# A gated retention layer with a ternary feed-forward on one core: Down's weights scaled by GpSimd alone and stored in more steps, another pace for one group's attention, and retention's norms in two lots

## The chip, the core and the metric

The kernel runs on one core of a Trainium2 chip. A core has five engines that run side by side and wait for one another only where data or buffers ask for it: TensorE (PE in the profile; PEld is its loading of weights), VectorE (DVE), ScalarE (ACT), GpSimd (POOL) and SyncE (SP), which issues most of the DMA transfers. Each engine works through its own instructions in a fixed order; an instruction that has to wait holds up all that stand behind it on that engine.

The metric is the time of one execution in microseconds on the device. Before the change it is 2254.69 us, the median of 3 runs (2254.12 to 2256.78).

## The reference

64 sequences of 128 tokens with 512 features pass through one layer. `k` and `v` of the attention are both the context `ctx`.

```python
def xattn(x, k, v, Wh, wg_w, wo_w, gn_gamma, gn_beta):      # 4 heads of 128
    Q, K, V = xh @ Wh, kh @ Wh, vh @ Wh                     # per head
    scores = einsum('bshe,bthe->bhst', Q, K) / sqrt(hd)
    masked = scores * Dn                                    # fixed decay masks
    A = maximum(abs(masked.sum(axis=0)), 1.0)               # summed over all 64 sequences
    O = einsum('hst,bthe->bshe', A, V).reshape(b, s, dim)
    Y = (O - mu) / sqrt(var + GN_EPS) * gn_gamma + gn_beta  # norm over the 512 features
    W = relu(x @ wg_w)
    return W * Y @ wo_w

def ffn(x, gate_w, up_w, down_w, gate_s, up_s, down_s):     # 512 -> 1408 -> 512
    g = (x @ gate_w.T) * gate_s
    u = (x @ up_w.T) * up_s
    return (silu(g) * u) @ down_w.T * down_s

x = x + tanh(g_xattn[0]) * xattn(layernorm(x), ctx, ctx, ...)
x = x + tanh(g_ffn[0]) * ffn(layernorm(x), ...)
```

The attention matrix `A` sums over all sequences before its absolute value is taken. So the scores of every sequence have to be there before any retention output can be made, and the kernel passes over the data twice.

## The kernel before

The 64 sequences are worked through in 16 groups of 4 (`NG`, `GB`), 512 tokens at a time. The large matrix products are done by a scheme in the manner of Strassen and Winograd: seven products of half-size blocks instead of eight, with sums and differences of the blocks formed beforehand (`combine_a` for weights, `combine_b` for tokens), and, for Down, sums of the weight tiles after a longer list (`W_SUMS`, `W_SUMS3`).

**Pass 1** (the loop over `g` that begins with `pending = None`) does for each group: `prepare` (the first layer norm; `bn` on VectorE, the power -1/2 on GpSimd in `inv_std`, then `xn`, a transpose on TensorE and a copy into `xnT`), `scores` for the group before, and `project` (the gate W) for the group before. Beside it runs `prepare_weights`, a generator that is asked once a group, from group 2 on (`next(weights, None)`), and that prepares the weights of pass 2 in nine parts: Wo (`load_wo`, `sum_wo`), five blocks of gate and up (`load_gu`, `sum_gu`; `NJ` is 5) and Down in three (`load_down`, `sum_down`). A part is loaded into one of two buffers (tag `raw`), summed on GpSimd, and stored to a scratch tensor in DRAM when the generator is asked the next time. In `sum_down`, L431 to L447, each of the 8 half tiles (6 in the third part) is first multiplied by Down's scale `ds`. Where `DOWN_SIGN` is positive, GpSimd does it (L436); where it is negative, VectorE does it with a factor of -1 (L438). GpSimd's 18 (or 12) sums follow; those beyond slot 15 go to the tile `more` (`dn_t` in the profile). The first two parts leave as two stores each (L481: `raw`, 2 MB, and `more`, 1.25 MB), the third as twenty stores of 128 KB (L487), with a pause after every seventh. What SP issues within one request stands behind the last load of `x` issued before (`tc.issue_after(last_load[0].ins)`); GpSimd's and VectorE's instructions are not bound in this way.

The tile `ds` shares its tag `wo`, with 3 buffers, with `gram`, `decay` and, in pass 2, with the loaded tiles `wo_w` (L727).

**Pass 2** runs, for each group, `ffn`, and beside it the attention of the next group (`attended`) and the retention of the group after that (`next_retention`, `retention`). `ffn` goes through a remainder block and then, for each of five blocks `j`, seven products in this order, with one `yield` after each: GS1 into `bank_f`; GA12 into `bank_a`, whose halves `hidden` (L879 on ScalarE, L880 on VectorE) turns into `h`; GS2 into `bank_c`; GA11 of the next block into `bank_a`; GS3, GS4 and GA22. After them come the 24 steps of Down (L1006). So `bank_a` is filled again two products after `hidden` began to read it.

`retention` makes four products (`po`, L652), copies them to `o`, normalises the four sequences (`bn` L251 and L252, `inv_std` L246 on VectorE and L247 on GpSimd, `normalised` L279, `square_transposed` L263), and sends the result through DRAM to turn it round (`moved`, L269 and L272). It then yields `WAIT` = 8 times, multiplies by gamma on ScalarE (L702), and multiplies W by it on GpSimd and VectorE (L711). `attended` makes seven products with Wo (L730), adds them to `x_t` (L741), and does the second layer norm in the same manner.

**The order of the work** has two sources. `interleave` mixes the generators: each has a number of steps, and the one whose next step is the smallest share of its number goes next. `ffn` has 50 (`FFN_STEPS`); the chain of attention and retention has `int(n_steps * 1.4)`. That is the order in which the program is written down. A planner then orders each engine's instructions by priority in that order, with durations of its own, so that an instruction can come earlier than it is written where its engine would otherwise be idle: the first load of Wo's weights, which belongs to pass 2, is issued at 243 us in the middle of pass 1.

In the first round of pass 2 (`g == 0`) the chain is longer: the rest of `retention` of group 1 (its four products are already done), `attended` of group 1, and `retention` of group 2.

Of the kernel before, what the change touches and what calls it, by code (L numbers as in the profile page):

```python
# [10 lines left out]
F32 = mybir.dt.float32  # L11
AF = mybir.ActivationFunctionType
ALU = mybir.AluOpType
# [22 lines left out]
DOWN_SIGN = (-1, -1, 1, 1, -1, 1, 1, 1)  # L36
# [84 lines left out]
def chain(*gens):  # L121
    for gen in gens:
        yield from gen
# [3 lines left out]
def flamingo_gated_layer(  # L127
# [21 lines left out]
    nc = tc.nc  # L149
    P = 128  # L150
    B, S, DIM = x.shape
# [8 lines left out]
    HN = DIM // 2  # L160
    KC = NC // 2
    NJ = NI // 2
# [179 lines left out]
    once = pass1.enter_context(tc.tile_pool(name="once", bufs=1))  # L342
# [39 lines left out]
    decay = att.tile([P, H, S], F32, tag="wo", name="decay", bufs=3)  # L382
    ds = att.tile([P, DIM], F32, tag="wo", name="ds", bufs=3)

    def constants():

        nc.sync.dma_start(out=ds, in_=down_s.partition_broadcast(P))
        nc.sync.dma_start(out=decay, in_=decayT)
        nc.sync.dma_start(out=gamma_sb, in_=gamma.rearrange("(c p) -> p c", p=P))
        nc.sync.dma_start(out=beta_sb, in_=beta.rearrange("(c p) -> p c", p=P))  # L390
        nc.sync.dma_start(out=gs_sb, in_=gate_s)
        nc.sync.dma_start(out=us_sb, in_=up_s)

        cols = slice(REST * P, INTER)
        for m, mat, k in ((GA11, gateT, 0), (GA12, gateT, 1), (7, upT, 0), (GA22, upT, 1)):
            nc.sync.dma_start(
                out=gu_rest[:, m],
                in_=mat[k * HN : (k + 1) * HN, cols].rearrange("(c p) i -> p c i", p=P),
            )
# [8 lines left out]
    def sum_wo(raw):  # L408

        nc.vector.tensor_scalar_mul(ds, ds, tanh_g[:, 1:2])  # L410
        nc.vector.tensor_scalar_mul(raw, raw, tanh_g[:, 0:1])
        t = once.tile([P, 4, KC, HN], F32, tag="sums", name="wo_t")
        b = (
            raw[:, 0:KC, 0:HN], raw[:, 0:KC, HN:DIM], raw[:, KC:NC, 0:HN], raw[:, KC:NC, HN:DIM],
        )
        combine_b(nc.gpsimd, [t[:, i] for i in range(4)], *b)
        return [
            (wo_scr[m], src)
            for m, src in zip(range(7), (b[0], b[2], b[3], t[:, 0], t[:, 1], t[:, 2], t[:, 3]))
        ]  # L420
# [10 lines left out]
    def sum_down(n, raw):  # L431

        for i in range(2 * len(DOWN_QUADS[n])):
            scale = ds[:, (i % 2) * HN : (i % 2 + 1) * HN]
            if DOWN_SIGN[i] > 0:
                nc.gpsimd.tensor_tensor(raw[:, i], raw[:, i], scale, ALU.mult)  # L436
            else:
                nc.vector.scalar_tensor_tensor(  # L438
                    raw[:, i], raw[:, i], -1.0, scale, ALU.mult, ALU.mult
                )  # L440
        more = once.tile([P, 10, HN], F32, tag="sums", name="dn_t")
        slots = [raw[:, i] for i in range(16)] + [more[:, i] for i in range(10)]
        sum_tiles(nc.gpsimd, slots, W_SUMS if n < 2 else W_SUMS3)
        if n == 2:
            rest_weights()
            return [(dn_scr[place, :, n], slots[i]) for i, place in W_PLACES3]
        return [  # L447
            (dn_scr[0:16, :, n].rearrange("m p e -> p m e"), raw),
            (dn_scr[16:26, :, n].rearrange("m p e -> p m e"), more),
        ]  # L450
# [20 lines left out]
    def prepare_weights():  # L471


        parts = [(load_wo, sum_wo)]
        parts += [(partial(load_gu, j), partial(sum_gu, j)) for j in range(NJ)]
        parts += [(partial(load_down, n), partial(sum_down, n)) for n in range(3)]
        raw, stores = parts[0][0](), []
        yield
        for n, (_, sums) in enumerate(parts):
            for dst, src in stores:  # L480
                nc.sync.dma_start(out=dst, in_=src)  # L481
            stores = sums(raw)
            if n + 1 < len(parts):
                raw = parts[n + 1][0]()
            yield
        for n, (dst, src) in enumerate(stores):
            nc.sync.dma_start(out=dst, in_=src)  # L487
            if n % 7 == 6:
                yield

    def rest_weights():
# [98 lines left out]
    pending = None  # L590
    weights = prepare_weights()
    for g in range(NG):
# [16 lines left out]
        steps = 3 if g == NG - 1 else 7  # L609
# [35 lines left out]
    def retention(g, v, ws):  # L645

        helper = nc.vector if g < 3 else nc.gpsimd

        o = att.tile([P, GB, H, P], F32, tag="yT", name="o")
        for h in range(H):  # L650
            po = ps_mm.tile([P, GB, P], F32, tag="mm", name="po")
            nc.tensor.matmul(  # L652
                po, lhsT=attn[:, h, :], rhs=v[:, h, :, :], start=True, stop=True
            )
            if h % 2:
                nc.vector.tensor_copy(o[:, :, h, :], po)
            else:
                nc.scalar.copy(o[:, :, h, :], po)
            yield
        if g:  # L660
            sq = att.tile([P, NQ, NC, GB, SQ], F32, tag="sq", name="sq")
        ons = []
        for j in range(GB):
            oj = o[:, j].rearrange("p h e -> p (h e)")
            mv = stat.tile([P, 2], F32, tag="mv", name="mv")
            bn(mv, oj)
            rs = stat.tile([P, 1], F32, tag="rs", name="rs")
            inv_std(rs, mv[:, 1:2], GN_EPS, 1)
            if g:
                square_transposed(sq, j, normalised(oj, mv[:, 0:1], rs))  # L670
            else:
                nc.vector.tensor_scalar(oj, oj, mv[:, 0:1], rs, ALU.subtract, ALU.mult)
                ons.append(oj)
        if g == 0:
            for q in range(2):
                tok = slice(q * HT, (q + 1) * HT)
                for d in range(2):
                    pt = ps_mm.tile([P, KC, HT], F32, tag="mm", name="pt")
                    for c in range(KC):
                        e = (d * KC + c) * P  # L680
                        for i in range(2):
                            nc.tensor.transpose(
                                pt[:, c, i * P : (i + 1) * P], ons[2 * q + i][:, e : e + P], ident
                            )
                    y = att.tile([P, KC, HT], F32, tag="xn", name="y", bufs=2)
                    for c in range(KC):
                        e = d * KC + c
                        nc.scalar.activation(
                            y[:, c, :], pt[:, c, :], AF.Identity,
                            scale=gamma_sb[:, e : e + 1], bias=beta_sb[:, e : e + 1],  # L690
                        )
                    (helper if d else nc.gpsimd).tensor_tensor(
                        ws[q][:, d], ws[q][:, d], y, ALU.mult
                    )
                    yield
            return
        yT = att.tile([P, NQ, NC, GB, SQ], F32, tag="yT", name="yT")
        moved(yT, sq, sq_scr[0][g % 2])
        for _ in range(WAIT):
            yield  # L700
        for e in range(NC):
            nc.scalar.activation(  # L702
                yT[:, :, e], yT[:, :, e], AF.Identity,
                scale=gamma_sb[:, e : e + 1], bias=beta_sb[:, e : e + 1],
            )
        yield
        for d in range(2):
            for q in range(2):
                for k in range(KC):
                    w = ws[q][:, d, k, :].rearrange("p (g i b) -> p i g b", i=NQ, b=SQ)  # L710
                    (helper if d else nc.gpsimd).tensor_tensor(  # L711
                        w, w, yT[:, :, d * KC + k, q * 2 : q * 2 + 2, :], ALU.mult
                    )
            yield
# [80 lines left out]
            moved(x1nT, sq, sq_scr[1][g % 2])  # L795

    WAIT = 8
    RET_STEPS = 4 + WAIT + 2
    ATT_STEPS = 8 + GB

    def new_x1nT():
# [256 lines left out]
    for g in range(NG - 1):  # L1058
        x_t = x_next.pop(0)
        x1nT = new_x1nT()  # L1060
        if g + 2 < NG:
            x_next.append(load_x(g + 2))
        steps = [attended(g + 1, x_t, ws, x1nT)] if g else [second]
        n_steps = ATT_STEPS + RET_STEPS
        if g == 0:
            steps.append(late_attended(1, x_t, x1nT))
            n_steps += RET_STEPS - 4
        if g + 2 < NG:
            steps.append(next_retention(g + 2))
        interleave(  # L1070
            (ffn(*pending), FFN_STEPS), (chain(*steps), int(n_steps * 1.4)),
        )
        with tc.issue_after(mid_down[0].ins):
            tokens = combine_tokens(nc.vector, x1nT)
        pending = (g + 1, x_t, x1nT, tokens)
# [59 lines left out]
```

## Time and profile before

| what | value |
|---|---|
| median of 3 runs | 2254.69 us (2254.12 to 2256.78) |
| the profiled execution's own time | 2253.64 us |
| its span, first to last instruction | 2251.8 us |
| busy: TensorE, VectorE, ScalarE, GpSimd | 2218.9, 1190.2, 603.3, 654.0 us |
| pass 1 up to the turn, 0 to 404 us: TensorE busy | 390.3 us |
| turn to pass 2, 404 to 440 us: TensorE busy | 32.7 of 36 us |
| a later group of pass 2, e.g. 624 to 738 us: TensorE busy | 113.3 of 114 us |
| GpSimd around the three parts of Down: 181 to 206, 206 to 230, 230 to 254 us | busy 20.7, 10.3, 18.0 us |

The profile is of one execution. A timeline row gives the start in us from the span's start, the duration in us, the engine, the line, the operation, the tile written and the tiles read, the shape, how many instructions are merged into the row (x8), and in brackets how long the engine was idle before it and what ended that. A row "A <- B: 9.6, 13, 0.9" among the waits says that A's engine was idle for B's sake for 9.6 us in total, 13 times, at most 0.9 us. In the chain of waits a row gives start, duration and what the last instruction was, at that time, waiting for. fp32 matmuls of 128x128 with 256 columns appear as two instructions each; within a row they start some 0.216 us apart, and a row of eight, one of the seven block products, is followed by the next 1.73 us after its start.

### The profile page before, as it was taken

To read this page: it belongs to the slowest core of one execution; us is meant where nothing else is said; L and a number is where in the kernel's file an instruction comes from. 1 tells how busy PE (TensorE), PEld (TensorE's weight loads), DVE (VectorE), ACT (ScalarE), POOL (GpSimd) and SP (SyncE) were. 2 spreads that over 40 slices of the span, in tenths; PEclk is the share of its full clock that TensorE was granted. 3 is DMA by queue.
4 is the path that set the end of the run, shared out by engine and by line. 5 is a ranking of instruction groups with operands and counts; after the bars stand their busy time and mean duration, and the time that the engine had idled before them with its cause. 6 is when DMAs were issued, how large, how long until landed. Compare 5 with 4: busy or idle time off the path is not lost.

```text
span 2251.8 us, 28752 instructions
## 1 busy us (share of the span) xinstructions
PE 2218.9 (99%) x10112; PEld 1889.7 (84%) x10112; DVE 1190.2 (53%) x2863; ACT 603.3 (27%) x1132; POOL 654.0 (29%) x1038
## 2 busy tenths in 40 slices
PE   8999999999999999999999999999999999999999
PEld 7878787778888888888888888888888888888888
DVE  6456543646454646464646464646464646454524
ACT  3444445322222222222222222222221212121221
POOL 4125300240323333333333333323232324141220
PEclk9999999999999999999999999999999999999999
DMA  9788855678777777777777777777777777766654
GB/s 300 263 279 308 287 190 176 253 240 260 255 269 240 265 249 256 258 248 266 247 267 236 257 247 266 239 262 243 268 237 269 236 272 233 280 205 243 223 184 145
DMA packets 216863, 558.46 MB, mean 248 GB/s; under 512 B 21264, under 2 KB 62992, under 8 KB 199952
## 3 DMA queue, kind: packets, MB, share of 16 engines
q1 hardware_dynamic: 211296, 539.58, 70.9%
q10 hardware_dynamic: 5424, 17.04, 2.0%
q8 instruction: 81, 1.33, 0.2%
q14 instruction: 62, 0.51, 0.1%
HBM read 454.31 MB, written 102.24 MB: 247 GB/s over the span
## 4 chain that ended last, share of the span: by engine, by line
PE 84%; DVE 6%; DMA 5%; POOL 3%; issue 1%; SPq 1%; ACT 0%; ACTq 0%; DVEq 0%; POOLq 0%
PE bank_c L287 18%; PE bank_a L287 12%; PE bank_c L1006 9%; PE bank_b L1006 6%; PE bank_f L287 6%; PE bank_b L287 6%; PE bank_f L1006 4%; PE bank_a L1006 4%; PE by L730 3%; PE sv L538 3%; PE bx L730 3%; PE bz L730 2%; PE po L652 2%; DMA gu_scr<-gu_raw 2%; DVE st L251 2%; PE bank_c L890 2%
## 5 line engine op out<-in xcount | busy, mean ns | idle before, releaser
L287 PE MATMUL bank_c<-tcomb,gu 128*128 128x256 f32 x1920 | 454.9, 380 | 0.7 <-DVE c L965 0.7
L287 PEld LDWEIGHTS bank_c<-tcomb,gu 128*128 128x128 f32 x1920 | 363.3, 190 | 59.3 <-issue 6.7
L335 POOL TENSOR_TENSOR h<-h 128x128 f32<-128x128 f32 x576 | 253.2, 470 | 398.5 <-DVE h L880 282.1
L287 PE MATMUL bank_a<-x1nT,gu 128*128 128x256 f32 x1280 | 305.5, 381 | 11.2 <-DVE h L880 9.6
L287 PEld LDWEIGHTS bank_a<-x1nT,gu 128*128 128x128 f32 x1280 | 241.8, 190 | 62.2 <-DVE h L880 14.8
L1006 PE MATMUL bank_c<-dn_w,h 128*128 128x256 f32 x896 | 211.7, 379 | 0.0
L1006 PEld LDWEIGHTS bank_c<-dn_w,h 128*128 128x128 f32 x896 | 170.2, 190 | 23.2
L879 ACT ACTIVATE sil<-c,gs_sb 128x256 f32<-128x256 f32 x176 | 89.3, 508 | 336.4 <-DVE c L965 171.7
L965 DVE TENSOR_TENSOR c<-bank_c,m 128x512 f32<-128x512 f32 x80 | 55.3, 691 | 219.5 <-PE bank_c L287 219.5
L247 POOL TENSOR_TENSOR rs<-ve,mhalf 128x1 f32<-128x1 f32 x128 | 73.4, 585 | 322.7 <-DVE ve L246 209.8
L711 POOL TENSOR_TENSOR w_t<-w_t,yT 128x256 f32<-128x256 f32 x112 | 91.6, 847 | 258.0 <-ACT yT L702 258.0
L741 POOL TENSOR_TENSOR x_t<-x_t,m 128x512 f32<-128x512 f32 x48 | 62.1, 1323 | 341.4 <-ACT m L751 341.4
L1006 PE MATMUL bank_b<-dn_w,h 128*128 128x256 f32 x640 | 156.4, 379 | 0.0
L335 DVE TENSOR_TENSOR h<-h 128x128 f32<-128x128 f32 x608 | 152.8, 312 | 4.3
L287 PE MATMUL bank_f<-tcomb,gu 128*128 128x256 f32 x640 | 151.2, 379 | 0.0
L287 PE MATMUL bank_b<-x1nT,gu 128*128 128x256 f32 x640 | 151.2, 379 | 0.0
L287 PEld LDWEIGHTS bank_b<-x1nT,gu 128*128 128x128 f32 x640 | 121.6, 190 | 22.1 <-issue 6.2
L287 PEld LDWEIGHTS bank_f<-tcomb,gu 128*128 128x128 f32 x640 | 121.6, 190 | 17.0 <-issue 0.5
L1006 PEld LDWEIGHTS bank_b<-dn_w,h 128*128 128x128 f32 x640 | 121.6, 190 | 16.5
L251 DVE BATCH_NORM_STATS2 st<-x_t 128x6 f32<-128x512 f32 x128 | 83.7, 682 | 79.3 <-DMA x_t<-in_x_dram 78.2
L538 PE MATMUL sv<-qw,c_t 128*128 128x256 f32 x512 | 122.0, 383 | 3.3 <-DVE xnT L513 3.3
L1026 DVE TENSOR_TENSOR x_t<-x_t,bank_c 128x256 f32<-128x256 f32 x192 | 77.8, 420 | 86.9 <-PE bank_c L1006 86.8
(150 smaller groups left out, 3260.8 us busy)
## 6 DMA issues: line engine op xcount, KB each, us to landing
dn_w<-dn_scr SPq DMA_DIRECT2D x320, 384.0 KB, 4.9
gu<-gu_scr SPq DMA_DIRECT2D x80, 1024.0 KB, 7.8
gu<-gu_scr SPq DMA_DIRECT2D x80, 768.0 KB, 5.9
x_t<-in_x_dram SPq DMA_DIRECT2D x62, 512.0 KB, 5.3
sq_scr<-sq SPq DMA_DIRECT2D x30, 1024.0 KB, 4.8
wo_w<-wo_scr SPq DMA_DIRECT2D x112, 256.0 KB, 3.6
dn_w<-dn_scr SPq DMA_DIRECT2D x96, 256.0 KB, 5.2
c_t<-in_ctxT_dram SPq DMA_DIRECT2D x64, 256.0 KB, 4.9
```

Source lines behind the costliest of these rows:

```text
L247: nc.gpsimd.tensor_tensor(dst, ve, mhalf[:, :n], ALU.pow)
L251: nc.vector.bn_stats(st, src)
L287: nc.tensor.matmul(out, lhsT=w[:, s, k, :], rhs=x_k, start=(start and s == 0 and k == 0), stop=(s == 1 and k == KC - 1), skip_group_check= ...
L335: engine.tensor_tensor(slots[to], slots[a], slots[b], ALU.add if sign == "+" else ALU.subtract)
L538: nc.tensor.matmul(sv[:, 0 : 2 + i : 1 + i, :], lhsT=c_t[j][:, h, :], rhs=qw[:, h, j : GB + 1 : GB - j, :], start=(i == 0), stop=(i == 1), ...
L711: (helper if d else nc.gpsimd).tensor_tensor(w, w, yT[:, :, d * KC + k, q * 2 : q * 2 + 2, :], ALU.mult)
L730: nc.tensor.matmul(bank[:, i * HN : (i + 1) * HN], lhsT=lhs[:, k, i * P : (i + 1) * P], rhs=w[:, k, :], start=(start and i == 0 and k == 0 ...
L741: engine.tensor_tensor(dst, dst, src.rearrange("p (b d) -> p b d", b=2), ALU.add)
L879: nc.scalar.activation(sil, gate, AF.Silu, scale=gs_sb[:, i : i + 1])
L965: nc.vector.tensor_add(c22, bank_c, m5)
L1006: last_down[0] = nc.tensor.matmul(places[acc], lhsT=hq[q][:, a, :], rhs=dn[n][:, q, :], start=start, stop=True, skip_group_check=True,)
L1026: add = nc.vector.tensor_tensor(dst, dst, places[acc], ALU.add if sign > 0 else ALU.subtract)
```

## The change

- In `sum_down` all half tiles are multiplied on GpSimd. A second tile, `minus_ds`, holds the negated scale; it is made once, in `sum_wo`, on VectorE. It lies in the pool `once` and not under the tag `wo`.
- In `prepare_weights` the two stores of Down's first part, and those of the second, are issued at two requests instead of one: the generator yields after the first of them. The twenty stores of the third part pause after every tenth instead of every seventh. The generator thereby has 14 steps instead of 13, for the 14 requests that pass 1 makes.
- In `retention`, for all groups but the first, a `yield` stands after the norms of the first two sequences, so that the four norms are written down in two lots with other work between them. `RET_STEPS` counts one more.
- The chain's number of steps in the first round of pass 2 is `int(37 * 1.05)` = 38 instead of `int(36 * 1.4)` = 50; in later rounds it is 37 instead of 36, by the additional step.

```diff
+    minus_ds = once.tile([P, DIM], F32, name="minus_ds")
...
     def sum_wo(raw):
 
         nc.vector.tensor_scalar_mul(ds, ds, tanh_g[:, 1:2])
+        nc.vector.tensor_scalar_mul(minus_ds, ds, -1.0)
...
     def sum_down(n, raw):
 
         for i in range(2 * len(DOWN_QUADS[n])):
-            scale = ds[:, (i % 2) * HN : (i % 2 + 1) * HN]
-            if DOWN_SIGN[i] > 0:
-                nc.gpsimd.tensor_tensor(raw[:, i], raw[:, i], scale, ALU.mult)
-            else:
-                nc.vector.scalar_tensor_tensor(
-                    raw[:, i], raw[:, i], -1.0, scale, ALU.mult, ALU.mult
-                )
+            scale = (ds if DOWN_SIGN[i] > 0 else minus_ds)[:, (i % 2) * HN : (i % 2 + 1) * HN]
+            nc.gpsimd.tensor_tensor(raw[:, i], raw[:, i], scale, ALU.mult)
...
         for n, (_, sums) in enumerate(parts):
-            for dst, src in stores:
+            for i, (dst, src) in enumerate(stores):
                 nc.sync.dma_start(out=dst, in_=src)
+                if n > NJ + 1 and i == 0:
+                    yield
             stores = sums(raw)
             if n + 1 < len(parts):
                 raw = parts[n + 1][0]()
             yield
         for n, (dst, src) in enumerate(stores):
             nc.sync.dma_start(out=dst, in_=src)
-            if n % 7 == 6:
+            if n % 10 == 9:
                 yield
...
             else:
                 nc.vector.tensor_scalar(oj, oj, mv[:, 0:1], rs, ALU.subtract, ALU.mult)
                 ons.append(oj)
+            if g and j == 1:
+                yield
         if g == 0:
...
     WAIT = 8
-    RET_STEPS = 4 + WAIT + 2
+    RET_STEPS = 5 + WAIT + 2
     ATT_STEPS = 8 + GB
...
         if g == 0:
             steps.append(late_attended(1, x_t, x1nT))
-            n_steps += RET_STEPS - 4
+            n_steps += RET_STEPS - 5
         if g + 2 < NG:
             steps.append(next_retention(g + 2))
         interleave(
-            (ffn(*pending), FFN_STEPS), (chain(*steps), int(n_steps * 1.4)),
+            (ffn(*pending), FFN_STEPS), (chain(*steps), int(n_steps * (1.4 if g else 1.05))),
         )
```

## The prediction

> **What bounds the kernel.** I read the page first (busy times), then TensorE's waits, then the timeline and the chain of waits around each of them, then SyncE's waits.
>
> ```profile
> PE 2218.9 (99%) x10112; PEld 1889.7 (84%) x10112; DVE 1190.2 (53%) x2863; ACT 603.3 (27%) x1132; POOL 654.0 (29%) x1038
> ```
>
> TensorE is the bound. No matmul is added or removed, so the change can only alter TensorE's idle time, some 33 us (2251.8 - 2218.9), and the half-speed matmuls that follow a long pause. TensorE's waits (who, for whom: us, times, longest):
>
> ```profile
> PE bank_a L287 <- DVE h L880: 9.6, 13, 0.9
> ...
> PE sv L538 <- DVE xnT L513: 3.3, 1, 3.3
> PE bx L730 <- POOL w_t L711: 2.5, 2, 1.5
> ```
>
> The other entries lie at the start, at the turn from pass 1 to pass 2, or are under 0.9 us. The three differ in kind.
>
> *The first comes once in each of 13 groups* (feed-forward of groups 1 to 13). Timeline of one:
>
> ```profile
> 734.12 1.30 DVE L263 STREAM_TRANSPOSE sq<-xn 128x512 f32<-128x512 f32 x2
> 734.68 1.89 PE L287 MATMUL bank_c<-tcomb,gu 128*128 128x256 f32 x8
> 734.95 0.47 ACT L879 ACTIVATE sil<-bank_a,gs_sb 128x256 f32<-128x256 f32 x1 [1.20 <-PE bank_a L287]
> ...
> 736.12 0.67 DVE L279 TENSOR_SCALAR xn<-o,mv,rs 128x512 f32<-128x512 f32 x1 [0.21 <-POOL rs L247]
> 736.77 0.47 DVE L880 SCALAR_TENSOR_TENSOR h<-bank_a,us_sb,sil 128x256 f32<-128x256 f32 x1
> 737.30 1.99 PE L287 MATMUL bank_a<-x1nT,gu 128*128 128x256 f32 x8 [0.72 <-DVE h L880]
> ...
> 738.47 0.67 DVE L279 TENSOR_SCALAR xn<-o,mv,rs 128x512 f32<-128x512 f32 x1 [0.61 <-POOL rs L247]
> ```
>
> A product takes 1.73 us from start to start (eight matmuls; neighbouring rows). `bank_a` could be refilled at 734.68 + 1.73 = 736.41, once VectorE's `h` has read it. `h` has its input at 735.42 (734.95 + 0.47) and takes 0.47, so starting by 735.9 costs nothing. It starts at 736.77, because the four norms of retention (L251 to L263) occupy VectorE from 728.98 to 739.9. TensorE loses 0.89 us, and 0.10 more in the product after the pause (1.83 to the next start): 0.99. In the first of the 13 groups the same rows give 1.21 (2.84 + 1.83 - 3.46). Together 12 x 0.99 + 1.21 = **13.1 us**.
>
> *The second comes once, in pass 1.* The chain of waits through it:
>
> ```profile
> 215.20 13.48 DMA dn_scr<-dn_raw
> ...
> 228.69 4.04 DMA dn_raw<-in_downT_dram
> ...
> 236.25 0.87 DVE dn_raw L438
> ...
> 245.34 6.01 DMA x_t<-in_x_dram
> ...
> 254.24 3.50 PE sv L538 x8
> ```
>
> Two stores of Down's first part leave together (2 MB and 1.25 MB). The load of the third part waits for their buffer, VectorE's negating multiply (L438) waits for the load, and all else of VectorE waits behind it. SyncE's waits show the next link:
>
> ```profile
> SPq L727 <- DVE dn_raw L438: 5.9, 1, 5.9
> SPq L727 <- POOL dn_raw L436: 5.8, 1, 5.8
> ```
>
> The first load of Wo's weights sits in SP's queue from 231.2 to 243.0, because its slot is that of `ds`, which the late multiplies still read; `x_t` and `c_t` queue behind it. TensorE loses 3.49 us before 254.24 (250.75 was possible), 1.61 because those eight matmuls run at half clock (3.34 to the next start instead of 1.73), and 0.77 and 0.61 at 235.36 and 241.58, where VectorE was late: **6.5 us**.
>
> *The third*, at 472 to 478, feed-forward of group 0: bx waits for gating on GpSimd behind eight sums, 1.20 + 1.63 us, 1.9 in slow matmuls after it; with 0.9 at 498, **5.6 us**.
>
> **The change, part by part.** *Scaling on GpSimd alone.* VectorE loses nine multiplies of 0.426 (median; 3.8 us) and their waits for loads (13.6 + 4.9 us in that line's waits). GpSimd gains 9 x 0.729 = 6.6 us (its like row; at the row's longest, 1.179, 10.6). One VectorE multiply for `minus_ds` (0.54, by the 128x512 row of L279) lies in the idle time before 60 us. The cover is GpSimd's idle time: 20.7 us busy of the 25 around Down's first part (181 to 206), under 6.1 in each of the groups before it. With three multiplies more that part needs about 23 of 24 us. What waits behind is `rstd` for the next group; at 200.91 it followed these sums and was first read at 209.3, so 2.2 us more are covered, and over 8 would show. I take 0; bounds: 0 to +2.
>
> [...]
>
> *Stores in more steps.* The generator is asked once a group, from group 2. Asked for the 9th time (group 10) it now issues only the 2 MB store; the 1.25 MB store and the third part's load come in group 11, the second part's stores in 12 and 13, and the twenty small ones as ten and ten in groups 14 and 15 (before: 7, 7, 6 in 12 to 14). Each batch stands in SP's queue behind that group's last `x_t` load, and all 14 requests are now used. So the load no longer waits for the buffer (5.2 us in SP's waits), the pair of stores no longer blocks SP (7.4 us for the issue at 216.04), and VectorE has nothing to wait for. Ten stores cost SP about ten times 0.8 to 1.1 us (rows L487, 6 of them took 8.0) and lie where only `x_t` for pass 2 follows. What is late next: `ds` is now held until the third part's multiplies near 250 to 260, so the hoisted Wo load can again block SP, but by the lag of a 1.25 MB store alone (some 5 us, against 12). Gain: all 6.5 at best; if the block keeps `x_t` late, VectorE waits for it again, and a wait of 5.6 cost 5.1 (row of 254.24), one of 6.2 cost 0.6 to 0.8 (TensorE's waits at 115 to 165). I leave 1.5 of it: **-5.0**; bounds -6.5 to 0.
>
> *Norms in two lots; the step counts.* Working the interleaving through by hand for groups 1 on: 28 pieces at 50/37 instead of 27 at 50/36. Retention's last product moves from behind the GS3 product to behind the next block's first one, 1.73 us earlier; the first lot stands behind GS3, the second behind the last product of the same block, just ahead of the block whose `h` is late. Norms can then start at about 727.0 instead of 728.98. The work that stood before `h` took 7.8 us, so it would end near 734.8 to 735.5, and `h` starts at about 736.0 behind one transpose: 0.1 us late, 0.2 with the slower first matmul. I take 0.3 a group: 13.1 - 13 x 0.3 = **-9.2**; bounds -13.1, and on the other side the first rival.
>
> *Another pace in group 0.* 40 pieces at 50/38: attention's first product moves from step 13 to 18, retention's products for group 2 from steps 24-27 to 32-36, its norms to 38 and 39 (the last of gate/up, the first of Down), its gating from 37-38 to 51-52. The cover is Down's 31 us; store of the norms to gamma took 21 us here (449.2 to 470.5), so bx of group 2, 5.2 us into the next feed-forward (562.51 - 557.33), keeps some 8 us. Uncovered, it would cost what bx did at 472, 4.7. The stall at 472 depends on data (gamma at 470.54 and the eight sums), not on pace, so I leave it: 0; bounds -5.6 to +4.7.
>
> **Sum.** -5.0 - 9.2 + 0 = -14.2. The profiled execution took 2253.64 us (span 2251.8), which gives 2239.4; it lies 1.05 under the median of the runs, 2254.69, so the forecast is **2240.5**, with its own range 2233 to 2247.
>
> **Rivals.** *A. The second lot takes the tight place (slower).* It stands directly ahead of `h`. If the transpose, xn and transpose still open at 735.46 all go first (0.70 + 0.67 + 0.71 = 2.08), `h` ends at 738.0 and TensorE loses 1.66 + 0.10 = 1.76 instead of 0.99: 13 x 0.77 = +10.0, with -5.0 from pass 1 +5.0: 2259.7. It decides against the change from 0.99 + 5.0/13 = 1.37 us a group on. For it: its place in the order; against: it waits for GpSimd's rs between pieces, and in such a hole `h` went at 736.77. *B. The steady stall stays* (the planner fills the earlier time with other work): -5.0, 2249.7. For it: VectorE has the same 11 us of work to place. *C. Pass 1's stall only moves with `ds`*: -9.2, 2245.5. For it: the slot is still shared. *D. Nothing moves*, because the planner orders by its own times (Wo's load at 243.01 is hoisted far): 2254.7. Against: SP's batches sat exactly at the requests, 7, 7 and 6.
>
> **Chances.** Forecast 0.43, A 0.21, B 0.15, C 0.14, D 0.07. A measurement of this kernel can tell about 0.2%, 4.5 us. Faster: 0.42 + 0.12 + 0.12 = 0.66; within: 0.01 + 0.02 + 0.03 + 0.02 + 0.05 = 0.13; slower: 0.19 from A and 0.02 from D. The range takes in A and, below, both stalls gone with a little of group 0's (-6.5 - 13.1 - 2): 2233 to 2260.
>
> **What would show it.** Right: no wait of `bank_a` for `h` over 0.3 us in groups 1 to 13 (period 113.2 to 113.5 instead of 114.13); no half-clock matmuls near 254; no wait of SP on the stores' buffer. Wrong: that wait at over 1.4 us, a Wo load that blocks SP for more than 6 us, or bx of group 2 waiting for `w_t`.

## The result and the profile after

| | before | after |
|---|---|---|
| median (range) of the runs compared | 2255.18 us (2254.12 to 2256.78, 4 runs, one more than in the table above) | 2319.7 us (2317.0 to 2320.34, 4 runs) |
| span of the profiled execution | 2251.8 us | 2315.1 us |
| round of group 0 in pass 2 | 123.9 us | 131.2 us |
| each of the next 13 rounds | 114.13 us (the first 114.35) | 119.14 us, three of them 117.5 |

The ratio is 1.0285, 95% interval 1.0268 to 1.0301: the change makes the kernel 2.85% slower. The forecast was 2240.5 us, faster. A round here runs from the first remainder product of one feed-forward (L892 after, L890 before) to the next. In the changed kernel all lines from L436 on stand two higher.

The page of the changed kernel, busy time of each engine:

```profile
PE 2243.5 (97%) x10112; PEld 1899.2 (82%) x10112; DVE 1177.6 (51%) x2855; ACT 601.7 (26%) x1132; POOL 656.1 (28%) x1047
```

TensorE has the same 10112 matmuls and is 24.6 us longer busy with them (2218.9 before): some run at half clock (granted clock 0.50 for 41.0 us in all, for 6.8 before). The rest of the loss is idle time. TensorE's waits:

```profile
PE bank_a L287 <- DVE h L882: 46.8, 27, 2.5
PE bank_b L1008 <- DMA dn_w<-dn_scr: 5.4, 1, 5.4
...
PE sv L538 <- DVE xnT L513: 1.0, 1, 1.0
PE bx L732 <- POOL w_t L713: 0.9, 2, 0.7
```

The wait of `bank_a` for `h`, which the change was forecast to shrink, went from 9.6 us in 13 waits to 46.8 us in 27, up to 2.5 us each. It now comes twice a round. The wait for Down's weights is new; the one of pass 1 (`sv`) and gating's (`bx`) shrank.

**The first of the two waits in a round** follows the second layer norm, in attention. Timeline of after (PE, DVE and POOL rows):

```profile
709.18 2.64 POOL L335 TENSOR_TENSOR h<-h 128x128 f32<-128x128 f32 x6 [2.30 <-DVE h L882]
709.75 1.29 DVE L251 BATCH_NORM_STATS2 st<-x_t 128x6 f32<-128x512 f32 x2
710.55 1.89 PE L287 MATMUL bank_a<-x1nT,gu 128*128 128x256 f32 x8
...
711.78 1.17 POOL L247 TENSOR_TENSOR rs<-ve,mhalf 128x1 f32<-128x1 f32 x2
...
712.37 1.16 DVE L279 TENSOR_SCALAR xn<-x_t,mv,rs 128x512 f32<-128x512 f32 x2 [0.93 <-POOL rs L247]
713.45 1.30 DVE L263 STREAM_TRANSPOSE sq<-xn 128x512 f32<-128x512 f32 x2
714.67 0.44 DVE L882 SCALAR_TENSOR_TENSOR h<-bank_a,us_sb,sil 128x256 f32<-128x256 f32 x1
715.16 1.99 PE L287 MATMUL bank_a<-x1nT,gu 128*128 128x256 f32 x8 [0.99 <-DVE h L882]
```

The same place before the change:

```profile
705.35 1.89 PE L287 MATMUL bank_a<-x1nT,gu 128*128 128x256 f32 x8
...
706.27 1.29 DVE L251 BATCH_NORM_STATS2 st<-x_t 128x6 f32<-128x512 f32 x2
...
707.88 0.47 DVE L880 SCALAR_TENSOR_TENSOR h<-bank_a,us_sb,sil 128x256 f32<-128x256 f32 x1
...
708.49 1.16 DVE L279 TENSOR_SCALAR xn<-x_t,mv,rs 128x512 f32<-128x512 f32 x2
```

Before, these two norms began 0.92 us after the product that `h` needs, and `h` stood ahead of `xn`. After, they begin 0.80 us before that product, and `h` stands behind both `xn` and both transposes. These norms are no part of the two lots: the chain's other step count has moved them.

**The second wait** is in retention's second lot:

```profile
739.42 1.89 PE L287 MATMUL bank_a<-x1nT,gu 128*128 128x256 f32 x8
...
740.05 3.04 POOL L335 TENSOR_TENSOR h<-h 128x128 f32<-128x128 f32 x7 [2.24 <-DVE h L882]
...
741.28 0.15 DVE L246 TENSOR_SCALAR ve<-mv 128x1 f32<-128x1 f32 x1
...
741.41 0.47 ACT L881 ACTIVATE sil<-bank_a,gs_sb 128x256 f32<-128x256 f32 x1 [1.20 <-PE bank_a L287]
...
743.05 1.17 POOL L247 TENSOR_TENSOR rs<-ve,mhalf 128x1 f32<-128x1 f32 x2
...
743.63 1.16 DVE L279 TENSOR_SCALAR xn<-o,mv,rs 128x512 f32<-128x512 f32 x2 [2.20 <-POOL rs L247]
744.71 1.30 DVE L263 STREAM_TRANSPOSE sq<-xn 128x512 f32<-128x512 f32 x2
745.93 0.44 DVE L882 SCALAR_TENSOR_TENSOR h<-bank_a,us_sb,sil 128x256 f32<-128x256 f32 x1
...
746.43 3.68 PE L287 MATMUL bank_a<-x1nT,gu 128*128 128x256 f32 x8 [2.53 <-DVE h L882]
```

`h` has its input at 741.88 (741.41 + 0.47), and VectorE is idle from 741.43 to 743.63. What stands next in its order is `xn`, whose `rs` (the power -1/2 of the norm) GpSimd makes only after seven sums that were queued earlier. `ve` was ready at 741.43, `rs` began at 743.05. Only after that, two `xn` and two transposes, comes `h`. And the eight matmuls behind the wait take 3.68 us instead of 1.89: half clock (granted 0.50 from 746.54 to 749.95).

**A round, accounted for.** From each matmul to the next lie 0.216 us where nothing disturbs. What one round has above that, from the start times (counted from the round's first remainder product); retention's matmuls of 512 columns, which take longer (`po` 0.592 us each in the median in both kernels, those of the seven products 0.379), are left out:

| kernel | excess, us (at) | sum | round |
|---|---|---|---|
| before | 0.88 + 0.10 (65.6) | 0.99 | 114.13 |
| after | 0.15 + 0.10 (30.4); 1.15 + 0.10 (38.5); 2.69 (69.8) + 1.77 of half clock | 5.96 | 119.14 |

Both leave about 113.15 us without any wait. So 13 rounds of 5.0 us more (three of them 3.3) make some 60 us; group 0's round adds 7.3 and the round after the 13 adds 1.5; pass 1 gives some 5 back.

**Group 0's round**, Down, timeline of after:

```profile
533.48 1.74 SPq L272 DMA_DIRECT2D yT<-sq_scr  x4
...
535.32 9.87 SPq L859 DMA_DIRECT2D dn_w<-dn_scr  x10
...
542.76 2.07 PE L1008 MATMUL bank_b<-dn_w,h 128*128 128x256 f32 x4 [5.38 <-DMA dn_w<-dn_scr]
```

Retention's store and its four loads for group 2 now meet Down, and TensorE waits 5.38 us for a tile of Down's weights, then runs at half clock (granted 0.50 from 541.74 to 548.57).

**Pass 1**: SyncE's waits show the sign that was named as wrong:

```profile
SPq L729 <- POOL dn_raw L438: 13.1, 1, 13.1
```

The hoisted Wo load blocks SP for 13.1 us, more than the two blocks of 5.9 and 5.8 before. Yet TensorE's wait behind it (`sv`) is 1.0 us instead of 3.3, with no half clock (the eight matmuls behind it take 1.99 us, 3.50 before).

### The profile page after: what moved, and what is told of

The parts are those of the page before. It is cut to its first block, busy times and chain, and to the rows that moved or that the text cites. A ratio compares the mean times of both kernels' runs of the same rounds, so it can differ in the third digit from the quotient of the medians.

```text
span 2315.1 us, 28773 instructions
## 1 busy us (share of the span) xinstructions
PE 2243.5 (97%) x10112; PEld 1899.2 (82%) x10112; DVE 1177.6 (51%) x2855; ACT 601.7 (26%) x1132; POOL 656.1 (28%) x1047
## 3 DMA queue, kind: packets, MB, share of 16 engines
q1 hardware_dynamic: 211296, 539.58, 69.8%
## 4 chain that ended last, share of the span: by engine, by line
PE 74%; DVE 12%; POOL 6%; DMA 4%; issue 1%; SPq 1%; ACT 1%; DVEq 0%; POOLq 0%; ACTq 0%
PE bank_c L287 15%; PE bank_a L287 12%; PE bank_c L1008 8%; PE bank_b L1008 6%; PE bank_b L287 5%; PE bank_f L287 4%; PE bank_a L1008 3%; PE bank_f L1008 3%; POOL h L335 3%; PE sv L538 3%; DVE sq L263 3%; DVE st L251 3%; POOL rs L247 2%; PE bx L732 2%; PE po L652 2%; PE bank_c L892 2%
## 5 line engine op out<-in xcount | busy, mean ns | idle before, releaser
L287 PE MATMUL bank_c<-tcomb,gu 128*128 128x256 f32 x1920 | 460.6, 383 | 0.0
L287 PEld LDWEIGHTS bank_c<-tcomb,gu 128*128 128x128 f32 x1920 | 369.4, 193 | 60.8 <-issue 6.7
L287 PE MATMUL bank_a<-x1nT,gu 128*128 128x256 f32 x1280 | 317.0, 392 | 48.4 <-DVE h L882 46.8
L335 POOL TENSOR_TENSOR h<-h 128x128 f32<-128x128 f32 x576 | 246.8, 460 | 351.2 <-DVE h L882 347.4
```

Source lines behind the costliest of these rows:

```text
L287: nc.tensor.matmul(out, lhsT=w[:, s, k, :], rhs=x_k, start=(start and s == 0 and k == 0), stop=(s == 1 and k == KC - 1), skip_group_check= ...
L335: engine.tensor_tensor(slots[to], slots[a], slots[b], ALU.add if sign == "+" else ALU.subtract)
```

## The experiments

Medians are beside runs of the kernel before on the same chip (its medians lay between 2254.83 and 2255.19 us). Each builds on the kernel before unless another is named.

**Pass 1's part alone**: `sum_down` and `prepare_weights` as changed, lots and counts as before.

> Only the part in pass 1 (Down's scaling on GpSimd, minus_ds, the stores in more steps); lots and paces as before. Theory: this part is a gain by itself, since the changed kernel reaches the first product of the remainder block 5.5 us earlier (434.1 against 439.6): 2249.5 us, groups of pass 2 still 114.13 us apart, no half-clock matmuls near 254. Rival: GpSimd's additional multiplies cost something later in pass 1 or in the feed-forward (Down's small stores now end one group later): 2254 us or more.

2250.37 us (2245.63 to 2254.68, 7 runs), ratio 0.9978 [0.9967, 0.9989]: 4.8 us gained, rounds of pass 2 unchanged at 114.13 us. In the profile `sv` waits 0.8 us and the half clock near 254 is gone, as the theory had it: the eight matmuls at 253.43 take 1.89 us.

**Two lots and a count of 37**, the rest as before:

```diff
+            if g and j == 1:
+                yield
...
-            (ffn(*pending), FFN_STEPS), (chain(*steps), int(n_steps * 1.4)),
+            (ffn(*pending), FFN_STEPS), (chain(*steps), 37 if g else 50),
```

> The kernel before with the yield between the norms alone, the chain counted as 37 steps in groups 1 on and 50 in group 0; pass 1 as before. Theory: the lots and the count by themselves make the two waits of bank_a for h in each group (1.0 and 2.5 us idle, then half-clock matmuls), 119.1 us a group instead of 114.1: 2255 + 13 x 5 = 2318 to 2320 us. Rival: group 0's pace puts the later groups into another phase that stays; then this kernel keeps 114.1 us a group and takes 2252 to 2256 us.

2319.04 us (2317.34 to 2320.38, 4 runs), ratio 1.028 [1.0263, 1.0298], +63.9 us: nearly the whole loss. TensorE's waits:

```profile
PE bank_a L287 <- DVE h L882: 47.0, 27, 2.5
```

**The count of 37 without the lots** (only the second hunk):

> The kernel before with the count alone, 37 instead of 36 steps in groups 1 on, no yield between the norms. Theory: the first of the two new waits (after the second layer norm's norms, about 1.0 us idle) comes from the count, because attention's last product is written one product earlier, so it shows here too, while the 2.5 us one does not: 1 to 1.3 us a group more than before, less what the norms gain by starting earlier; 2255 to 2272 us. Rival: the yield does everything: only the old wait of 0.7 us or none, 2242 to 2256 us.

2268.09 us (2265.53 to 2270.03, 4 runs), ratio 1.0056 [1.0041, 1.0071], +12.9 us. TensorE's waits:

```profile
PE bank_a L287 <- DVE h L880: 14.0, 14, 1.0
```

These are the waits after attention's norms. Its round by start times: 0.26 (30.4) + 1.26 (38.5) + 0.32 (67.3) = 1.84, 114.98 us. The old wait at 65.6 has shrunk from 0.99 to 0.32, as forecast for the earlier products of retention; a new one of 1.26 stands 29 us ahead of it.

**The lots with the old count of 36**:

```diff
+            if g and j == 1:
+                yield
...
+            (ffn(*pending), FFN_STEPS), (chain(*steps), 36 if g else 50),
```

> The kernel before with the yield between the norms, but the chain still counted as 36 steps from group 1 on (group 0 as before, 50). Theory: the yield's place just ahead of the block's h makes the 2.5 us wait, whatever the count; the wait after the second layer norm's norms (1.0 us) comes from the count and is not here: 117 to 118.5 us a group, 2290 to 2312 us. Rival: the count of 37 makes both; then one wait of 0.7 us as before or less, 2243 to 2258 us.

2249.19 us (2247.27 to 2250.77, 9 runs), ratio 0.9971 [0.9961, 0.9981]: 5.6 us faster. Here my theory, that the lots alone make the 2.5 us wait, fell, and its rival held. Timeline:

```profile
737.02 2.71 POOL L335 TENSOR_TENSOR h<-h 128x128 f32<-128x128 f32 x6
...
739.74 0.55 POOL L247 TENSOR_TENSOR rs<-ve,mhalf 128x1 f32<-128x1 f32 x1
739.74 0.45 DVE L882 SCALAR_TENSOR_TENSOR h<-bank_a,us_sb,sil 128x256 f32<-128x256 f32 x1
...
740.25 2.00 PE L287 MATMUL bank_a<-x1nT,gu 128*128 128x256 f32 x8
740.33 0.55 DVE L279 TENSOR_SCALAR xn<-o,mv,rs 128x512 f32<-128x512 f32 x1
```

One step earlier or later in the interleaving decides which goes first. Here GpSimd's sums have just ended when `rs` is asked for, and `h` stands ahead of the second lot's `xn`. A round loses 0.42 us and takes 113.56.

**After, with `rs` ahead of the sums**: GpSimd's sums of `h` may not pass the last `rs`.

```diff
+        last_rs[0] = nc.gpsimd.tensor_tensor(dst, ve, mhalf[:, :n], ALU.pow)
...
+                    with tc.issue_after(last_rs[0].ins):
+                        sum_tiles(e, h_slots[q], (one,))
```

> The changed kernel with one thing more: GpSimd's sums of h (some_sums in ffn) are put behind the last rs written before them, on GpSimd's own queue; the work is the same. Theory: the 2.5 us wait is VectorE standing 2.2 us before xn for an rs that GpSimd makes only after seven sums (3.0 us), with h queued behind xn; with rs first the xn comes 1.5 to 1.9 us earlier, the wait falls to 0.7 to 1.0 us and the half-clock matmuls go, and the first wait of 1.0 us falls to 0.4 to 0.7: some 116 us a group, 2270 to 2290 us. Rival: VectorE's own norm work ahead of h makes the wait; then it stays at 118 to 119 us a group, 2305 to 2320 us.

2271.81 us (2268.9 to 2272.27, 4 runs), ratio 1.0073 [1.0058, 1.0088]: 48 us of the loss are gone, with counts and lots as in after. TensorE's waits:

```profile
PE bank_a L289 <- DVE h L884: 17.7, 27, 0.7
```

Both waits are still there, but none is over 0.7 us; by start times a round loses 0.88 us at the first (1.25 in after) and 0.96 at the second (4.46 in after, half clock included). That `rs` queues behind sums is therefore what makes the second wait long; `h` behind the norms makes it at all.

**After, with only the two counts put back** (36, and 50 for group 0):

```diff
-            (ffn(*pending), FFN_STEPS), (chain(*steps), int(n_steps * (1.4 if g else 1.05))),
+            (ffn(*pending), FFN_STEPS), (chain(*steps), 36 if g else 50),
```

> The changed kernel with only its two step counts put back (36 for groups 1 on, 50 for group 0); pass 1's part and the two lots stay. Theory (the counts, not the lots, make the loss: 2.5 us of wait twice a group come from the count of 37 meeting the second lot): pass 1's -4.8 and the two lots' -6.0 at 36 add up, 2243 to 2246, no wait of bank_a for h over 0.3 us in the steady groups. Rival (the parts do not add: with pass 1's new order the planner places the lots otherwise): a wait of bank_a for h of 0.7 us or more a group stays, 2250 or more.

2242.55 us (2241.4 to 2247.97, 5 runs), ratio 0.995 [0.9938, 0.9962]. TensorE's waits:

```profile
PE bank_a L287 <- DVE h L882: 0.2, 1, 0.2
```

Two integers are worth 77 us. The lots and pass 1's part together gain 12.4 us, a little more than their 4.8 + 5.6.

**Group 0's pace alone**: count 37 for group 0, 36 for the others, one lot.

> The kernel before with group 0's slower pace alone (37 steps for its 38 pieces). Theory: the turned norms of group 2 stand in SP's queue ahead of Down's weights (yT waits for its own store, ten loads of dn_w behind it), TensorE waits some 5.4 us for dn_w in group 0's Down and runs at half clock after it, less the smaller wait of bx: +6 to +8, 2261 to 2263 us, later groups 114.1 us apart. Rival: that wait comes from the changed stores or lots; then 2252 to 2256 us.

2261.42 us (2259.61 to 2264.49, 6 runs), ratio 1.0029 [1.0017, 1.0041], +6.2 us. Group 0's round takes 131.3 us, the others 114.13. In Down TensorE waits 3.4 us for `dn_w`, 1.6 for `h`, 1.4 for `x_t`. With the two larger parts this adds up: -4.8 + 63.9 + 6.2 = +65.3, against +64.5 measured.

**The same, with group 2's store and four loads on ScalarE's queue** (`moved` with `nc.scalar` for `g == 2`):

> The kernel before with group 0's slower pace alone (2261.4 us), and the turning of group 2's retention through DRAM (one store, four loads) issued from ScalarE's queue instead of SP's. Theory: SP's wait for that store, with Down's weights queued behind it, is what makes TensorE wait 3.4 us for dn_w; it goes, with the half-clock matmuls after it: 2255 to 2258 us; what stays are the two waits for VectorE in Down (1.6 and 1.4 us). Rival: dn_w is late because of VectorE or of the transfers themselves; unchanged at 2260 to 2263 us.

2261.45 us (2255.2 to 2264.32, 10 runs), ratio 1.0025 [1.0014, 1.0035]: nothing gained in the median. TensorE's timeline of the run before this one, with its wait for `dn_w`, and of this one:

```profile
548.61 2.90 PE L1006 MATMUL bank_f<-dn_w,h 128*128 128x256 f32 x6 [3.37 <-DMA dn_w<-dn_scr]
```

```profile
559.40 1.10 PE L1007 MATMUL bank_b<-dn_w,h 128*128 128x256 f32 x4 [1.76 <-DMA dn_w<-dn_scr]
```

The wait at 548.61 and the half clock behind it (six matmuls in 2.90 us; such a row takes 1.46 in this run) went, and the profiled group 0's round fell from 131.3 to 129.1 us. But the waits for `x_t` rose to 2.3 us, and another wait for `dn_w` came 11 us later. The chain of waits that ends with a load of this window shows slow ones just before it:

```profile
544.68 6.84 DMA dn_w<-dn_scr
...
551.59 8.47 DMA dn_w<-dn_scr
```

Over the whole run such loads take 5.0 us in the median (384 KB). So my theory that the store and the loads stand in the way in SP's queue holds at most for the first wait.

**Count 44 for group 0**: retention's norms for group 2 then come before Down.

> Before with the count of group 0 at 44 instead of 50 (37 gave 2261.4): retention's norms for group 2 then come in the last of gate/up and not with Down's first steps. Theory (the 6 us at 37 are the meeting of these norms, and of the loads behind them, with Down's weights, which TensorE then waits for): no wait of Down for dn_w over 1 us and 2253 to 2256. Rival (the later pace itself, by any amount, moves a load of SP's queue ahead of dn_w): a wait for dn_w of 2 us or more and 2258 to 2262.

2255.75 us (2253.76 to 2257.82, 11 runs), ratio 1.0004 [0.9995, 1.0013]; no wait for `dn_w`, group 0's round 124.1 us. Loads of `dn_w` are slow here too (those of 384 KB take 6.3 us in the median from 515 to 555 us, against 4.3 in the kernel before), but none is waited for. Not the later pace as such costs, nor a slow load as such, but the meeting of these norms and transfers with Down.

**Scaling alone** (stores as before) and **stores alone** (VectorE still multiplies):

> The first half of pass 1's part alone: all of Down's scaling on GpSimd (with minus_ds), stores as before. Theory (the gain of 4.8 us of pass 1 belongs to the stores, since the load of the third part waits for its buffer whoever multiplies): only VectorE's two late starts at 235 and 241 can go (0.77 + 0.61 = 1.4 us), the sv product before 254 keeps a wait near 3.3 us and its half-clock matmuls: 2253.5 to 2255. Rival (VectorE's wait for the load was the cause, and x_t was late only through it): the sv wait falls under 1 us and the time is near 2250.

> The other half alone: the stores in more steps, VectorE still multiplies. Theory (the stores are the cause): the sv wait falls to about 1 us, as with both halves (2250.4), so 2250 to 2251.5. Rival (GpSimd's scaling does it): the sv wait stays near 3.3 us, 2254 to 2255.

Scaling alone: 2257.54 us (2255.59 to 2263.08, 11 runs), ratio 1.0013 [1.0004, 1.0022], slower, where I had expected a little faster. Stores alone: 2248.34 us (2246.93 to 2250.51, 9 runs), ratio 0.9968 [0.9958, 0.9977]. The chain of waits of scaling alone, and the row of SyncE's waits behind it:

```profile
251.35 6.29 DMA x_t<-in_x_dram
...
260.54 3.78 PE sv L536 x8
```

```profile
SPq L725 <- POOL dn_raw L438: 13.9, 1, 13.9
```

GpSimd reaches the third part's six multiplies only after its sums of the second part, at 241.95, and ends them at 248.07. The Wo load, which waits for `ds`, leaves at 248.10 instead of 243.01, `x_t` behind it at 251.35 instead of 245.34, and `sv` waits 7.6 us instead of 3.3. The profiled execution was the slowest of the eleven (2263.08 us), so these rows show the way of the loss and overstate its size. So the stores are the gain and the scaling is a small loss; with the stores in more steps it is hardly to be told (2250.37 with it, 2248.34 without; the intervals overlap). The 2.6 us that the scaling lost came through the Wo load and `x_t`.

**A version that beats both**: pass 1's part, count 36 and group 0's old pace, lots from group 3 on; the second lot may not pass the `h` it would delay, and retention waits two steps less afterwards.

```diff
+            if lots and j == 2:
+                yield
+                yield
+            if lots and j >= 2:
+                with tc.issue_after(last_h[0].ins):
+                    norm(j)
...
-        for _ in range(WAIT):
+        for _ in range(WAIT - 2 * lots):
...
-            nc.vector.scalar_tensor_tensor(
+            last_h[0] = nc.vector.scalar_tensor_tensor(
```

> The kernel with the pass 1 part alone (2250.4 us), and from group 3's retention on the norms in two lots, but with two yields between them and the second lot's VectorE instructions put behind the h of the next block's GA12 product; two fewer empty waits after, count 36. Theory: what costs is a lot of norms ahead of that h; behind it there is a whole block of 12 us for them, so the wait of 0.7 us goes: 113.1 to 113.4 us a group, 2250.4 - 13 x 0.9 = 2238 to 2240 us. Rival: VectorE has too much to do in these blocks, and the wait turns up at the next block's h or at the gating: 114 us a group or more, 2249 us or more.

2236.92 us (2235.43 to 2238.81, 4 runs), ratio 0.9921 [0.9907, 0.9936]. Timeline:

```profile
732.15 0.48 DVE L893 SCALAR_TENSOR_TENSOR h<-bank_a,us_sb,sil 128x256 f32<-128x256 f32 x1 [0.66 <-ACT sil L892]
732.55 1.28 DVE L251 BATCH_NORM_STATS2 st<-o 128x6 f32<-128x512 f32 x2
...
733.11 1.89 PE L287 MATMUL bank_a<-x1nT,gu 128*128 128x256 f32 x8
```

`h` goes first by order, `bank_a` waits for nothing, and a round takes 113.14 us: 0.99 less than before.

## Why the prediction was wrong

**Pass 1: right.** Forecast -5.0, measured -4.8. Its make-up was a little off: the stores alone bring -6.6, all of the 6.5 that the two stalls cost, and the scaling, taken at 0 (bounds 0 to +2), costs 2.6 alone, since GpSimd was not free when the third part arrived. The two misses cancel, so that -4.8 lies so close to -5.0 is in part luck. Rival C's sign came (a block of 13.1 us), but `x_t` was issued 9.1 us before the product that needs it could have begun (264.12, 273.20), where before it was 5.4 (245.34, 250.75). So 1.2 us were lost behind it instead of 3.5, and nothing to half clock. The block of 13.1 us in the queue cost only what it made late.

**Norms in two lots: the step that failed.** The prediction put it: "Norms can then start at about 727.0 instead of 728.98 [...] I take 0.3 a group", -9.2. Measured with both its parts: +63.9; instead of 0.3 us a round lost 5.96. The start of the norms was about right; three other things were wrong.

1. *Only the named work was followed through the interleaving.* The working had the 28 pieces at 37 right for retention: its products do come earlier, and with the count alone the old wait shrinks to 0.32 us. But the count moves every piece of the chain. Attention's second pair of norms moved too, from 0.92 us behind the product that `h` needs to 0.80 ahead of it, and made a new wait of 1.26 us. Lots at 36, count at 37, and both cost -5.6, +12.9 and +63.9: some 57 us belong to neither part but to their meeting.
2. *The wait for `rs` was taken as a hole for `h`.* Rival A had the right mechanism, "The second lot takes the tight place", but priced it at 2.08 us of VectorE's own work, and held against itself that `h` could go while VectorE waits for GpSimd's `rs`. Here `h` stood behind both `xn`, so VectorE idled 2.20 us, 1.75 of them with `h`'s input ready. The rival left out what makes that wait long: seven sums of 0.43 us ahead of two tiny powers. With `rs` ahead of them 48 us return.
3. *A long pause was priced as a short one.* 0.10 us was added for the matmuls after a wait of 0.7 us. After one of 2.5 us it is 1.8 in ten of 13 rounds. It was in the prediction's own rows: 1.61 us after the 3.3 us wait in pass 1.

**Group 0's pace: wrong.** Taken at 0, with Down's 31 us named as the cover. Measured +6.2, beyond the bound of +4.7. The cover did hold for what it was named for, `bx` of group 2, which does not wait. What was left out is that the norms and transfers themselves would meet Down's own. The stall at 472 was said not to depend on the pace; it did shrink, 2.5 to 0.9 us. Why `dn_w` arrives late there is settled only in part: with the transfers on another queue the first wait and its half clock go, but another wait comes behind loads that take longer, and the median gains nothing.

**The price of the old wait, 0.99 us a group, was right**: with it gone entirely the round went from 114.13 to 113.14. The target was real, only the change did not hit it.

## What to carry to other kernels

A step count in a proportional interleaving moves all of a generator's work: list what stands ahead of each tight instruction before and after, not only the work that the change is about, and try the count and the structure apart. Where an operation must go first, say so in the order instead of hoping for a count: `rs` ahead of the sums returned 48 us with the counts as they were, and with the old counts the version that orders `h` first takes 2236.9 us, where the one that leaves it to the count takes 2242.6. Before work is put ahead of a critical instruction, ask what that work itself waits for on other engines: here VectorE idled 2.20 us for `rs`, with `h` queued behind, and TensorE waited 2.53 us for `h`.

## What was not expected of the hardware

In the changed kernel the half clock after a pause came on a time grid of its own. The same wait of 2.53 us returns 13 times. Time from start to start for the following matmuls, four at a time (0.86 us at full clock, 1.71 at half):

| wait ends at, us | first four | next | next | next |
|---|---|---|---|---|
| 746.43 | 1.79 | 1.71 | 0.88 | 0.86 |
| 865.56 | 1.47 | 1.71 | 1.20 | 0.86 |
| 984.70 | 1.15 | 1.71 | 1.52 | 0.86 |
| 1103.84 | 0.97 | 1.57 | 1.71 | 0.99 |
| 1222.99 | 0.97 | 1.26 | 1.71 | 1.31 |
| 1342.14 | 0.97 | 0.86 | 0.86 | 0.86 |

The slow stretch always costs 1.69 us beyond the 0.11 of the first start, so it is some 3.4 us long. It begins 0.32 us later from round to round, against the wait, and in three of 13 rounds does not come at all; those are the rounds of 117.5 us. Waits of 0.99 us were never followed by it.

The granted clock in the trace of after shows the grid itself: it is 0.50 for 3.41 us at a time, from 746.54, 866.00, 985.47, 1104.94 and 1224.40 us on, 119.47 us apart whatever the wait does. A round takes 119.14, so the stretch comes 0.33 later against the wait from round to round. Laid end to end from one of these starts to the next, 35 stretches of 3.41 us fill the 119.47. Counted in such stretches, the 13 long waits part cleanly: ten put 2.0 us or more of their idle time into one stretch, and the next ran at half clock; three put 1.9 us or less into any one, and it did not. What makes the clock do so is not shown here.
